# Scans of a four-block image network: where layer norm's factors, their third tile and the squares of x2 are computed

## The chip, the cores and the metric

The kernel runs on one core of a Trainium2 chip, as one program. The metric is device time in microseconds (us), as the median of several executions. The engines are named as the profile names them: PE (TensorE: matmuls, and PEld for its weight loads), DVE (VectorE), ACT (ScalarE), POOL (GpSimd) and SP (SyncE, which issues most DMAs). Each engine takes its own instructions strictly in their order; semaphores join them.

## What is computed

Four residual blocks follow each other on x of 32 x 192 x 56 x 56 numbers in float32: attention with agents, two scans over the pixels (this case), a shift with a small convolution, and a long convolution. The block of the scans, cut to what matters:

```python
k, v, r = (einsum('btc,dc->btd', gn(x), W) for W in (Wk, Wv, Wr))    # b images, t = 3136 pixels, c = 192
x_fwd = wkv_scan(-exp(w_decay), u, k, v)         # y_t = (p + e^(u+k) v) / (q + e^(u+k)), p and q decayed sums
x_bwd = flip(wkv_scan(-exp(w_decay), u, flip(k), flip(v)))
h = sigmoid(r) * 0.5 * (x_fwd + x_bwd)
h = (h - mean_c(h)) * rsqrt(var_c(h) + 1e-5) * ln_g + ln_b           # layer norm over the 192 channels
x2 = x + einsum('btc,dc->btd', h, Wo)            # the next block's group norm needs x2's sums and squares
```

## The kernel before

All of it is in `scan_pairs`. The 32 images are taken as 16 pairs. A pair's 2 x 192 channels lie on three tiles of 128 rows: the first 128 channels of image 0 (tile 0), those of image 1 (tile 1), and the last 64 channels of both, 64 rows each (tile 2, the "third tile"). The 3136 pixels are cut into four pieces m of 784, so one tile is 128 x 784. For a matmul over all channels `_Pairs.outer` (L870) makes tiles 0 and 1, `_Pairs.inner` (L881) the third.

The loop at L1237 runs over the pairs p and, inside, over four steps i. One step does three things:
- `backwards(s, m)` (L1152) for the pair's piece m, from the last piece to the first. For each tile it forms the gate g from Wr (ACT: L1163, L1167, L1168), scans the numerator p and the denominator q from right to left (DVE: two scans L1107, then two scalar_tensor_tensor L1109, here called STT), inverts q on ACT (`inverse`: Ln at L1114, Exp at L1115) and forms h on DVE (L1171 multiplies p by the inverse, L1172 adds the forward part, L1173 multiplies by g).
- `finish` (L1175) for the piece that the step before completed: centred h by PE, its squares on ACT (L1186), their channel mean by PE (`outer` with `mean_w`, so that the mean of both images stands on all 128 rows of two PSUM tiles), the logarithm of variance plus epsilon on ACT (L1195: two of 128 rows for tiles 0 and 1, and two of 64 rows that put the third tile together from both), the exponential that makes it the factor (L1205, three tiles), Wo by PE, the product of both on DVE (L1206), x2 and its sums on DVE (L1207), x2's squares summed on ACT (L1212, into `squares`), and the store of x2 (L1215).
- `forwards(ahead, i)` (L1124) for the next pair's piece i: keys e^k from PSUM on ACT (L1138), values (L1143), the forward scan of the same form, and its quotient y (L1150).

Once in a pair, `moments_of` reads the sums and squares (L1068, L1069), and `conclude` (L1217) finishes the group norm's factors and compares 60 kept maxima with bounds (five L1229, then L1230 takes the smallest).

The order of instructions on each engine is not that of the source: a scheduler orders them when the program is built, by the order of the source and by modelled readiness. It is fixed from then on. PSUM holds four tiles of two banks for all matmuls of the stage (`turned`, L912). SBUF tiles come from pools: x has 7 buffers, ek 12, and g, sq and rd share 8 under the tag "t".

Of the kernel before, what the change touches and what calls it, by code (L numbers as in the profile page):

```python
# [28 lines left out]
C = 192  # L29
# [7 lines left out]
MC = 784  # L37
# [802 lines left out]
class _Pairs:  # L840
# [3 lines left out]
    def __init__(self, nc, pool):  # L844
        self.nc, self.pool = nc, pool

    def blocks(self, name, ap):

        nc = self.nc
        aa = self.pool.tile([128, 128], F32, name=f"{name}_aa", tag=f"{name}_aa")  # L850
        ca = self.pool.tile([128, 128], F32, name=f"{name}_ca", tag=f"{name}_ca")
        ac = self.pool.tile([128, 64], F32, name=f"{name}_ac", tag=f"{name}_ac")
        cc = self.pool.tile([128, 128], F32, name=f"{name}_cc", tag=f"{name}_cc")
        nc.gpsimd.memset(cc, 0.0)  # L854
        nc.sync.dma_start(out=aa, in_=ap[0:128, 0:128])
        nc.sync.dma_start(out=ac, in_=ap[0:128, 128:C])
        for r in (slice(0, 64), slice(64, 128)):
            nc.sync.dma_start(out=ca[r], in_=ap[128:C, 0:128])
            nc.sync.dma_start(out=cc[r, r], in_=ap[128:C, 128:C])
        return aa, ca, ac, cc  # L860
# [32 lines left out]
def scan_pairs(ctx: ExitStack, tc: tile.TileContext, a, k, x1, st_a, st_c, x2, rs2, wogT, count):  # L893
# [6 lines left out]
    NB = x1.shape[0]  # L900
    cp = ctx.enter_context(tc.tile_pool(name="s_c", bufs=1))
    kp = ctx.enter_context(tc.tile_pool(name="s_k", bufs=3 * NM))
    wp = ctx.enter_context(tc.tile_pool(name="s_w", bufs=8))
    sp = ctx.enter_context(tc.tile_pool(name="s_s", bufs=2))
    pp = ctx.enter_context(tc.tile_pool(name="s_p", bufs=4, space=PSUM))
    pairs = _Pairs(nc, cp)
# [10 lines left out]
        return [t[:, h * HM : (h + 1) * HM] for h in range(2)]  # L917


    wo = [small("wo_a", [128, C]), small("wo_c", [64, C])]  # L920
    lg = [small("lg_a", [128, 1]), small("lg_c", [64, 1])]
    lb = [small("lb_a", [128, 1]), small("lb_c", [64, 1])]
    cen = [small("cen_a", [128, C]), small("cen_c", [64, C])]
    for i, r in enumerate((slice(0, 128), slice(128, C))):
        nc.sync.dma_start(out=wo[i], in_=a["L1_conv_WoT"][r])
        nc.sync.dma_start(out=lg[i], in_=a["L1_conv_ln_g"][r].unsqueeze(1))
# [10 lines left out]
    for i, r in enumerate((slice(0, 128), slice(128, C))):  # L937
        n = (128, 64)[i]
        ps, _, _ = turned()
        for s in range(2):  # L940
            nc.tensor.matmul(ps[:n, 0, :C], cen[s][:, r], wo[s], start=(s == 0), stop=(s == 1))
        turn = wp.tile([128, C], F32, name="turn", tag="turn", bufs=1)
        nc.vector.tensor_copy(turn[:n], ps[:n, 0, :C])
        nc.sync.dma_start(out=wogT[r], in_=turn[:n])

    wk, wv, wr = (blocks(n, a[f"L1_conv_{n}T"]) for n in ("Wk", "Wv", "Wr"))
    wog, centre, mean_w, group = (
        blocks("wog", wogT), blocks("cen", k["centre"]), blocks("mean", k["mean192"]), blocks("grp", k["group192"])
    )
    wd = pairs.vector("wd", a["L1_conv_w_decay"])  # L950
    eu = pairs.vector("eu", a["L1_conv_u"])
# [23 lines left out]
    nc.vector.memset(eps, 4.0 * LN_EPS)  # L975
    kept_a, kept_c = small("kept_a", [128, 2, NB // 4, 2]), small("kept_c", [128, 2, NB // 4])
    fine = small("fine", [128, NB // 2])

    def of(t):
        return slice(0, 1) if t < 2 else slice(1, 2)  # L980
# [140 lines left out]
                nc.gpsimd.memset(s, 0.0)  # L1121
        return carry

    def forwards(s, m):  # L1124
        s.ek[m] = [kp.tile([128, MC], F32, name="ek", tag="ek") for _ in range(3)]
        s.bv[m] = [kp.tile([128, MC], F32, name="bv", tag="bv") for _ in range(3)]
        s.y[m] = [kp.tile([128, MC], F32, name="y", tag="y", bufs=3 * NM + 4) for _ in range(3)]
        xn = normed(s, m)
        for tiles in ((0, 1), (2,)):
            for wt in (wk, wv):  # L1130
                ps = [turned() for _ in tiles]
                if len(tiles) == 2:
                    pairs.outer(wt, [q[2] for q in ps], xn)
                else:
                    pairs.inner(wt, ps[0][2], xn)
                for t, (_, both, _) in zip(tiles, ps):
                    if wt is wk:
                        nc.scalar.activation(  # L1138
                            s.ek[m][t].rearrange("p (h n) -> p h n", h=2), both, AF.Exp,
                            accum_out=s.seen[:, 0, 3 * m + t : 3 * m + t + 1],  # L1140
                        )
                    else:
                        nc.vector.tensor_tensor(  # L1143
                            s.bv[m][t].rearrange("p (h n) -> p h n", h=2), both,
                            s.ek[m][t].rearrange("p (h n) -> p h n", h=2), ALU.mult,
                        )
            for t in tiles:
                num, den = scan(s, m, t, s.fore, False)
                inverse(s, den, m, t, 1)
                nc.vector.tensor_tensor(s.y[m][t], num, den, ALU.mult)  # L1150

    def backwards(s, m):  # L1152
        xn = normed(s, m)
        h = s.y[m]
        for tiles in ((0, 1), (2,)):
            ps = [turned() for _ in tiles]
            if len(tiles) == 2:
                pairs.outer(wr, [q[2] for q in ps], xn)
            else:
                pairs.inner(wr, ps[0][2], xn)  # L1160
            for t, (_, both, _) in zip(tiles, ps):
                g = wp.tile([128, MC], F32, name="g", tag="t")
                nc.scalar.activation(  # L1163
                    g.rearrange("p (h n) -> p h n", h=2), both, AF.Exp, scale=-1.0,
                    accum_out=s.seen[:, 3, 3 * m + t : 3 * m + t + 1],
                )
                nc.scalar.activation(g, g, AF.Ln, bias=1.0)  # L1167
                nc.scalar.activation(g, g, AF.Exp, scale=-1.0)  # L1168
                num, den = scan(s, m, t, s.back, True)
                inverse(s, den, m, t, 2)  # L1170
                nc.vector.tensor_tensor(num, num, den, ALU.mult)  # L1171
                nc.vector.tensor_tensor(h[t], h[t], num, ALU.add)  # L1172
                nc.vector.tensor_tensor(h[t], h[t], g, ALU.mult)  # L1173

    def finish(s, m):  # L1175
        h, xs = s.y[m], load(s.p, m)
        hs = [parts(t) for t in h]
        sq = [wp.tile([128, MC], F32, name="sq", tag="t") for _ in range(3)]
# [12 lines left out]
        pv = [turned() for _ in range(2)]  # L1191
        pairs.outer(mean_w, [q[2] for q in pv], sqs)
        rds = [wp.tile([128, MC], F32, name="rd", tag="t") for _ in range(3)]
        for r, t, i, _ in places:
            nc.scalar.activation(rds[t][r].rearrange("p (h n) -> p h n", h=2), pv[i][1][r], AF.Ln, bias=eps[r])  # L1195
        for tiles in ((0, 1), (2,)):
            po = [turned() for _ in tiles]
            if len(tiles) == 2:
                pairs.outer(wog, [q[2] for q in po], hs)
            else:  # L1200
                pairs.inner(wog, po[0][2], hs)
            for t, (_, out, _) in zip(tiles, po):
                rd = rds[t]
                rdh = rd.rearrange("p (h n) -> p h n", h=2)
                nc.scalar.activation(rd, rd, AF.Exp, scale=-0.5)  # L1205
                nc.vector.tensor_tensor(rdh, out, rdh, ALU.mult)  # L1206
                nc.vector.scalar_tensor_tensor(  # L1207
                    xs[t], rd, cb[:, of(t)], xs[t], ALU.add, ALU.add, accum_out=s.sums[:, t, m : m + 1]
                )
                if m == NM - 1:  # L1210
                    nc.vector.tensor_scalar(s.away[:, t], s.sums[:, t, m : m + 1], -1.0 / MC, None, ALU.mult)
                nc.scalar.activation(rd, xs[t], AF.Square, bias=s.away[:, t], accum_out=s.squares[:, t, m : m + 1])  # L1212
        rows = slice(m * MC // S, (m + 1) * MC // S)
        for r, t, i, c in places:
            nc.sync.dma_start(out=x2[c, i, rows, s.p], in_=xs[t][r].rearrange("p (h w) -> p h w", w=S))  # L1215

    def conclude(s):  # L1217
        p = s.p
# [6 lines left out]
        for r, t, i, c in places:  # L1225
            nc.sync.dma_start(out=x2[c, i, S, p], in_=row[r, t])

        for i, top in enumerate((1e8, 1e15, 1e15, 1e15, 1e30)):
            nc.vector.tensor_scalar(s.seen[:, i, :], s.seen[:, i, :], top, None, ALU.is_lt)  # L1229
        nc.vector.tensor_reduce(fine[:, p : p + 1], s.seen.rearrange("p a b -> p (a b)"), AX.X, ALU.min)  # L1230

# [3 lines left out]
    for p in range(NP):  # L1237
        ahead = State(p + 1) if p + 1 < NP else None
        for i in range(NM):
            m = NM - 1 - i  # L1240
            backwards(s, m)
            if i > 0:
                finish(s, m + 1)
            elif before is not None:
                finish(before, 0)
            if ahead is not None:
                forwards(ahead, i)
            if before is not None:
                if i == 1:
                    before.spread = deviations(*moments_of(before), sp, "2")  # L1250
                elif i == 2:
                    conclude(before)
        before, s = s, ahead
    finish(before, 0)
    before.spread = deviations(*moments_of(before), sp, "2")
    conclude(before)
    nc.sync.dma_start(out=rs2[0:128], in_=kept_a)
# [4 lines left out]
    nc.vector.tensor_scalar(eu, eu, 1e8, None, ALU.is_lt)  # L1262
    bad = small("bad", [128, 1])
    nc.vector.tensor_reduce(bad, fine, AX.X, ALU.min)
    nc.vector.tensor_tensor(bad, bad, eu[:, 0:1], ALU.mult)
    nc.vector.tensor_tensor(bad, bad, eu[:, 1:2], ALU.mult)
    nc.vector.tensor_scalar(bad, bad, -1.0, 1.0, ALU.mult, ALU.add)
# [572 lines left out]
```

## Time and profile before

| what | us |
|---|---|
| median of 3 runs (12514.6 to 12529.47) | 12525.27 |
| the profiled execution's own time | 12522.92 |
| its span, first to last instruction | 12521.1 |
| stage of the scans, about 5065 to 8580 of the span | 3515 |
| one step of the stage (53 steps in 5400 to 8300) | 54.7 |
| DVE busy in 7000 to 8000 of the span | 951.9 of 1000 |
| ACT busy there | 670.4 |
| PE busy there | 841.6 |

The page gives busy time in tenths for 40 equal slices of the span; the stage of the scans is slices 17 to 27. A view by windows gives busy time in chosen stretches, a view of waits lists for which instruction of which engine another stood still, and a timeline lists instructions in order of time, with the idle time before each in brackets and the instruction that ended it.

### The profile page before, as it was taken

The page shows a single profiled execution, that of the slowest core. Times are in us where ns is not written, and L with a number is a line of the kernel's source. Part 1 is how long each engine was busy: PE and PEld are TensorE (multiplying, and loading weights), DVE is VectorE, ACT ScalarE, POOL GpSimd, SP SyncE. Part 2 cuts the span into 40 slices and gives each one's busy share as a digit, 9 for nine tenths or more (in the row PEclk, how much of TensorE's full clock was granted, in tenths as well). Part 3 has the DMA queues.
Part 4 walks back from the last instruction along what each step waited for, and adds up shares of the span by engine and source line. Part 5 has one row for each costly group of instructions (what it writes and reads, how often), then busy time and mean ns, then how long its engine had stood idle before and what let it go on. Part 6 is the DMA issues. An engine that isn't in the chain of part 4 may idle for free. (4 is left out here: it accounts for less than half of the span.)

```text
span 12521.1 us, 164987 instructions
## 1 busy us (share of the span) xinstructions
PE 11416.7 (91%) x62738; PEld 7090.4 (57%) x62738; DVE 10875.9 (87%) x15618; ACT 6374.2 (51%) x12012; POOL 2177.8 (17%) x2238
## 2 busy tenths in 40 slices
PE   4999999999999999788888888887999999999999
PEld 1555555555555555333333333335777777777777
DVE  3888888888888888899999999997888888888888
ACT  2555555555555555566666666664333333333333
POOL 0000000000000000555555555552000000000000
PEclk7999999999999999899999999998999999999999
DMA  2111111111111111233333333332111111111111
GB/s 65 36 45 40 40 40 40 39 44 54 40 40 39 40 40 40 74 93 85 86 93 90 83 92 93 86 86 75 43 45 41 44 42 43 43 42 44 42 43 29
DMA packets 930936, 693.89 MB, mean 55 GB/s; under 512 B 775551, under 2 KB 817002, under 8 KB 921121
## 3 DMA queue, kind: packets, MB, share of 16 engines
q1 hardware_dynamic: 930136, 683.25, 21.0%
q8 instruction: 500, 8.19, 0.3%
q14 instruction: 300, 2.45, 0.1%
HBM read 403.18 MB, written 240.80 MB: 51 GB/s over the span
## 5 line engine op out<-in xcount | busy, mean ns | idle before, releaser
L591 DVE SCALAR_TENSOR_TENSOR o<-v_a,dww,o 128x896 f32<-128x896 f32 (+1 forms) x1024 | 1054.0, 1029 | 408.0 <-ACT v_a L565 291.8
L1766 ACT COPY y<-ps 64x252 f32<-64x252 f32 (+1 forms) x2376 | 808.2, 340 | 1134.9 <-PE ps L1760 1104.4
L1684 PE MATMUL ps<-f,real 84*84 84x112 f32 x6144 | 1090.8, 259 | 0.0
L1684 PE MATMUL ps<-f,imag 84*84 84x112 f32 x6144 | 1089.4, 259 | 0.0
L1691 ACT COPY z<-ps 84x448 f32<-84x448 f32 x768 | 405.6, 528 | 1218.0 <-PE ps L1684 1216.4
L1684 PEld LDWEIGHTS ps<-f,real 84*84 84x84 f32 x6144 | 783.9, 153 | 134.2 <-issue 95.8
L854 POOL MEMSET Wk_cc<- 128x128 f32 x1 | 0.2, 204 | 4812.1 <-DVE ones L1269 4812.1
L1684 PEld LDWEIGHTS ps<-f,imag 84*84 84x84 f32 x6144 | 763.8, 153 | 0.0
L1114 ACT ACTIVATE q<-q 128x784 f32<-128x784 f32 x384 | 329.0, 857 | 746.2 <-DVE q L1109 684.3
L591 DVE SCALAR_TENSOR_TENSOR o<-v_c,dww,o 128x448 f32<-128x448 f32 (+1 forms) x1024 | 635.2, 620 | 5.2
L604 PE MATMUL ps<-xs_a,gk_a 128*98 128x448 f32 (+1 forms) x1536 | 639.6, 497 | 0.0
L608 ACT ACTIVATE pr<-ps,low 98x896 f32<-98x896 f32 (+1 forms) x384 | 352.2, 917 | 557.0 <-DVE low L606 557.0
L605 PE MATMUL ps<-xs_c,gk_c 125*98 125x448 f32 (+1 forms) x1536 | 633.1, 493 | 0.0
L696 PE MATMUL ps<-gq_a,xs_a 128*112 128x294 f32 x1792 | 600.5, 416 | 18.8 <-DVE pq L701 18.8
L1701 PE MATMUL ps<-z,f 84*114 84x448 f32 x1536 | 608.9, 539 | 0.0
L697 PE MATMUL ps<-gq_c,xs_c 125*112 125x294 f32 x1792 | 592.9, 411 | 0.0
L1550 POOL TENSOR_TENSOR mat<-tap,tap 114x114 f32<-114x114 f32 x96 | 40.9, 426 | 3166.3 <-PE ps L1610 2313.0
L876 PE MATMUL ps<-sq,mean_aa 128*128 128x392 f32 x512 | 309.2, 748 | 258.6 <-ACT sq L1186 256.6
L1658 PE MATMUL re<-y,f 128*84 128x420 f32 (+1 forms) x1152 | 532.0, 542 | 8.7 <-ACT y L1766 7.6
L709 ACT ACTIVATE pq<-pq 112x1176 f32<-112x1176 f32 x224 | 265.3, 1184 | 530.4 <-DVE pq L701 406.5
L1760 PEld LDWEIGHTS ps<-f,padded 114*128 114x128 f32 x3168 | 473.1, 192 | 96.4 <-issue 70.3
L1658 PE MATMUL im<-y,f 128*84 128x420 f32 (+1 forms) x1152 | 526.9, 538 | 0.0
(398 smaller groups left out, 29528.0 us busy)
## 6 DMA issues: line engine op xcount, KB each, us to landing
x<-x SPq DMA_DIRECT2D x512, 392.0 KB
x<-x SPq DMA_DIRECT2D x512, 196.0 KB
x<-x SPq DMA_DIRECT2D x192, 399.0 KB
out_x<-x SPq DMA_DIRECT2D x384, 196.0 KB
x_a<-in_x SPq DMA_DIRECT2D x32, 1568.0 KB
x<-x_a SPq DMA_DIRECT2D x32, 1568.0 KB
x_c<-in_x SPq DMA_DIRECT2D x64, 392.0 KB
x<-x_c SPq DMA_DIRECT2D x64, 392.0 KB
```

The lines of the kernel that those rows point to most:

```text
L591: nc.vector.scalar_tensor_tensor(dst, tap(i), dww[:, t, i : i + 1], dst, ALU.mult, ALU.add)
L604: mm(ps[P2, h, :n], g[:, cols], xs_a[j][:, px], start=True, stop=False)
L605: mm(ps[P2, h, :n], gk_c[0:KC, 2 * j + h, cols], xs_c[j][0:KC, px], start=False, stop=True)
L608: nc.scalar.activation(pr[:, :, :n], ps[P2, :, :n], AF.Exp, bias=low[:, j, p : p + 1], accum_out=sums[:, j, p : p + 1])
L696: mm(ps[:SUB, i, :HA], xs_a[j][:, px], g, start=True, stop=False)
L697: mm(ps[:SUB, i, :HA], xs_c[j][0:KC, px], gq_c[0:KC, 2 * j + (q + i) // ns], start=False, stop=True)
L1658: nc.tensor.matmul(ps[:, : n * 84], f2[:, i, :], y[:, i0 : i0 + n].rearrange("p g s u -> p (g s u)"), start=True, stop=True)
L1684: nc.tensor.matmul(ps[:84, i * 2 * S : (i + 1) * 2 * S], part[:, i0 + i].rearrange("p s u -> p (s u)"), f3[:, m, :], start=(m == 0), stop= ...
L1691: nc.scalar.copy(z[:, i0 : i0 + n].rearrange("p g m w -> p (g m w)"), ps[:84, : n * 2 * S])
L1701: nc.tensor.matmul(got, f4[:, m, :], z[:, i0 : i0 + n, m, :], start=(m == 0), stop=(m == 1))
L1760: nc.tensor.matmul(ps[:, g * 168 : (g + 1) * 168], flat[:, (g0 + g) * 128 : (g0 + g + 1) * 128], f1, start=True, stop=True)
L1766: nc.scalar.copy(y[64 * m : 64 * m + 64, 2 * g0 + i : 2 * (g0 + n) : 2], got[64 * i : 64 * i + 64, :, :, m, :])
```

## The change

Nothing changes in what is computed. In the loop, `backwards` and `finish` become generators that are advanced in turn: the pair's tiles 0 and 1 backwards, then `finish` up to the factors, then the third tile backwards, then the rest of `finish`. The third tile's factors are no longer computed: the exponentials of tiles 0 and 1 are taken at once, after each logarithm over all 128 rows, and two DMAs on ACT's queue copy rows 0 to 63 of the first and rows 64 to 127 of the second into the third tile. `finish` returns the three squares of x2 uncomputed, and `forwards` issues them behind the first two keys. The product of L1206 goes to the buffer of sq. The five comparisons and the minimum of `conclude` become one instruction with a count. Pool "t" has 9 buffers, ek 13; weights that are used only once are held in "t"; two blocks of `mean_w` that nobody reads are not loaded.

```diff
-    def forwards(s, m):
-        s.ek[m] = [kp.tile([128, MC], F32, name="ek", tag="ek") for _ in range(3)]
+    def forwards(s, m, behind=()):
+        s.ek[m] = [kp.tile([128, MC], F32, name="ek", tag="ek", bufs=3 * NM + 1) for _ in range(3)]
...
+                if wt is wk and tiles == (0, 1):
+                    for later in behind:
+                        later()
...
     def backwards(s, m):
...
                 nc.vector.tensor_tensor(h[t], h[t], g, ALU.mult)
+            yield
...
     def finish(s, m):
...
         rds = [wp.tile([128, MC], F32, name="rd", tag="t") for _ in range(3)]
-        for r, t, i, _ in places:
-            nc.scalar.activation(rds[t][r].rearrange("p (h n) -> p h n", h=2), pv[i][1][r], AF.Ln, bias=eps[r])
+        for t, (_, both, _) in enumerate(pv):
+            nc.scalar.activation(rds[t].rearrange("p (h n) -> p h n", h=2), both, AF.Ln, bias=eps)
+            nc.scalar.activation(rds[t], rds[t], AF.Exp, scale=-0.5)
+
+        for t, r in enumerate((slice(0, 64), slice(64, 128))):
+            nc.scalar.dma_start(out=rds[2][r], in_=rds[t][r])
+        yield
+        left = []
         for tiles in ((0, 1), (2,)):
...
-                nc.scalar.activation(rd, rd, AF.Exp, scale=-0.5)
-                nc.vector.tensor_tensor(rdh, out, rdh, ALU.mult)
+                nc.vector.tensor_tensor(
+                    sq[t].rearrange("p (h n) -> p h n", h=2), out, rds[t].rearrange("p (h n) -> p h n", h=2), ALU.mult
+                )
                 nc.vector.scalar_tensor_tensor(
-                    xs[t], rd, cb[:, of(t)], xs[t], ALU.add, ALU.add, accum_out=s.sums[:, t, m : m + 1]
+                    xs[t], sq[t], cb[:, of(t)], xs[t], ALU.add, ALU.add, accum_out=s.sums[:, t, m : m + 1]
                 )
...
-                nc.scalar.activation(rd, xs[t], AF.Square, bias=s.away[:, t], accum_out=s.squares[:, t, m : m + 1])
+                def square(t=t):
+                    nc.scalar.activation(
+                        sq[t], xs[t], AF.Square, bias=s.away[:, t], accum_out=s.squares[:, t, m : m + 1]
+                    )
+                left.append(square)
...
+        yield left
...
     def conclude(s):
...
-        for i, top in enumerate((1e8, 1e15, 1e15, 1e15, 1e30)):
-            nc.vector.tensor_scalar(s.seen[:, i, :], s.seen[:, i, :], top, None, ALU.is_lt)
-        nc.vector.tensor_reduce(fine[:, p : p + 1], s.seen.rearrange("p a b -> p (a b)"), AX.X, ALU.min)
+        nc.vector.scalar_tensor_tensor(
+            s.seen, s.seen, 1.0, tops, ALU.mult, ALU.is_lt, accum_out=fine[:, p : p + 1]
+        )
...
         for i in range(NM):
             m = NM - 1 - i
-            backwards(s, m)
+            back, ending = backwards(s, m), None
             if i > 0:
-                finish(s, m + 1)
+                ending = finish(s, m + 1)
             elif before is not None:
-                finish(before, 0)
+                ending = finish(before, 0)
+            next(back)
+            if ending is not None:
+                next(ending)
+            next(back)
+            left = next(ending) if ending is not None else []
             if ahead is not None:
-                forwards(ahead, i)
+                forwards(ahead, i, left)
```

## Prediction

> **What bounds the kernel now.** I read the slices first, then busy time by windows in the stage of the scans, then the DVE's waits there, then the timelines of DVE and ACT around each wait. In the slices (tenths busy) the scans are slices 17 to 27. The window's columns are its length, then busy us and instructions of PE, PEld, DVE, ACT and POOL, the granted clock, the DMA share and GB/s.
>
> ```profile
> DVE  3888888888888888899999999997888888888888
> ACT  2555555555555555566666666664333333333333
> ```
> ```profile
> 7000.00:8000.00 1000.00, 841.60 (x2965) 372.96 (x2966) 951.91 (x993) 670.40 (x1126) 525.63 (x501) 0.92 0.36 89
> ```
>
> DVE works 951.9 of 1000 us, PE 841.6, ACT 670.4. So the stage lasts as long as DVE's instructions plus the time DVE stands still. Over 5400 to 8300 (53 steps, 13.25 pairs) its waits are few and named (us in total, times, longest); line numbers are those of the kernel before throughout:
>
> ```profile
> DVE p L1171 <- ACT q L1115: 83.7, 53, 2.3
> DVE q L1107 <- ACT ek L1138: 32.7, 31, 1.2
> DVE mv L1069 <- ACT rd L1212: 12.4, 13, 1.0
> ```
> ```profile
> L1109 DVE SCALAR_TENSOR_TENSOR q<-ek,eu,q 128x784 f32<-128x784 f32 x318 | 324.8, 1025 | 8.7 <-POOL f L1121 0.5
> ```
>
> Per pair that is 6.3 us at L1171, 2.5 at the key scan, 0.95 at L1069, and 0.65 in gaps before an L1109 that follows its own scan directly: 10.4 us, or some 160 us in the stage. This is all that the change can win. The first wait, in one step (DVE, then ACT):
>
> ```profile
> 6037.27 1.04 DVE L1109 SCALAR_TENSOR_TENSOR q<-ek,eu,q 128x784 f32<-128x784 f32 x1
> 6038.22 0.97 DVE L1173 TENSOR_TENSOR y<-y,g 128x784 f32<-128x784 f32 x1
> 6039.10 0.32 DVE L1229 TENSOR_SCALAR seen<-seen 128x12 f32<-128x12 f32 x3
> 6039.34 0.20 DVE L1230 TENSOR_REDUCE fine<-seen 128x1 f32<-128x60 f32 x1
> 6040.87 0.98 DVE L1171 TENSOR_TENSOR p<-p,q 128x784 f32<-128x784 f32 x1 [1.33 <-ACT q L1115]
> ```
> ```profile
> 6038.35 0.86 ACT L1114 ACTIVATE q<-q 128x784 f32<-128x784 f32 x1
> 6039.11 0.89 ACT L1195 ACTIVATE rd<-ps,eps 64x784 f32<-64x784 f32 x1
> 6039.91 0.84 ACT L1115 ACTIVATE q<-q 128x784 f32<-128x784 f32 x1
> ```
>
> DVE hands over the third tile's denominator at 6038.25 and gets the inverse at 6040.87: 2.6 us through Ln, one foreign instruction, Exp. DVE has one 0.88 us instruction to fill them. The second wait: the squares stand ahead of the keys.
>
> ```profile
> 6049.34 0.94 ACT L1212 ACTIVATE rd<-x,away 128x784 f32<-128x784 f32 x1
> 6050.19 0.19 ACT L1212 ACTIVATION_READ_ACCUMULATOR rd<-x,away 128x1 f32 x1
> 6050.40 0.82 ACT L1138 ACTIVATE ek<-ps 128x784 f32<-128x784 f32 x1
> ```
>
> **The change, part by part.** Which instruction fills a wait is decided by the compiled order, which is known for the changed kernel (it has no times). I take spacings from the timelines: scan 1.76 us, STT 0.94, tensor_tensor 0.88, Ln or Exp 0.76, a square with its accumulator 1.1 before a dependent.
>
> *L1171 of the third tile.* In the new order L1173 of tile 1 moves ahead of the last L1109, so it no longer fills the wait; one L1206 takes its place. ACT's order across the wait is L1114, L1167, L1115: again one foreign instruction (0.75 against 0.80 us), so the 2.6 us stay. By the pair's four steps: step 0 has L1206 and the new count (0.2, as L1230) and waits 2.6 - 0.88 - 0.2 = 1.5; step 1 has L1206 and a tiny L1037, 1.6; step 3 L1206 alone, 1.7; step 2 has L1173, the copy of L1224 and two L1206, 2.85 in all, and waits 0. Sum 4.8 against 6.3: 1.5 us per pair won. The change covers this wait in one step of four, not in all.
>
> *Squares.* In the new ACT order two of the three squares still precede the keys in all steps, but one L1206 and one L1207 now follow tile 1's sums on DVE, where mostly one L1207 followed. With tile 1's sums ready at X, the square takes 1.1, the key 0.95 to its reader: the scan can start at X + 2.1. DVE is free at X + 0.95 before (wait 1.15; the trace has 1.15 in each of 26 such steps) and at X + 1.83 after: 0.3. Step 0 adds L1068: 0.05. Step 2 has ACT late by 0.7 us from normalising x (L1089), but L1173 too behind X: 0.2. Step 1 needs L1211 of tile 1, which the new order puts behind the last L1206: 1.0. Sum 1.5 against 2.5: 1.0 won.
>
> *L1069* follows four scan and STT instructions, over 5 us, in the new order; its wait, 0.95 per pair, goes. *L1109*: both scans come before both STTs in every step; the 0.65 goes. The count that replaces L1229 and L1230 lies mostly in the wait just summed; only one L1229 stood outside: 0.1.
>
> Sum: 1.5 + 1.0 + 0.95 + 0.65 + 0.1 = 4.2 us per pair. Some 14.5 of the 16 pairs have this form (the first lacks `finish`, the last `forwards`): 61 us. The set-up loads three blocks less (0.43 + 0.54 + 0.59 on SP) but SP waits up to 1 us longer at the second store of wogT: 0.5, rounded away.
>
> *ACT's work.* Removed per step: two Ln of 64 rows, 0.90 each, and one Exp, 0.84. This frees 2.6 of 54.7 us on an engine that idles for a third: nothing by itself. If it had no idle time left, it would be worth 2.6 us per step.
>
> *The two DMAs on ACT's queue.* No DMA of ACT's is in the trace; the nearest row is SP's loads of x (L997): 319 ns least, 522 median, 1694 most; SP's worst x2 store took 2157. I take 0.5 each. A gain is excluded, since they only add. They wait for the Exp ahead of them, and behind them on ACT stands L1163 of the third tile, then the Ln of L1114 that DVE awaits. From the moment tile 0's denominator is done (0): L1114, L1168, L1115 to 2.6, three L1186 to 5.3, tile 1's inverse 6.4 to 8.25, the mean by PE to 7.9, two Ln to 10.0, two Exp to 11.6; DMAs at 11.8; L1163 is done 1.1 us after them, at about 14. DVE, with 12 instructions between, ends the third denominator at 16.1. Room for both issues together: 3.2 us; in the step kind where one L1186 falls behind tile 1's Ln, 2.1. At 0.5 each it is covered; at 1694 each (3.4) it would cost 0.2 to 1.3 us per step.
>
> A rule speaks against them. The Trainium skill, DMA: Bandwidth & Descriptors, section Rules for kernel authors, says that two transfers to disjoint partition halves do not run side by side but one after the other. The nearest row is wogT (96 KB): issued 5016.25, released its waiter at 5017.99, 1.7 us. Each half here is 200 KB: by the row 1.7 to 3.5 us for both in parallel, by the rule twice that, at most 7. The third tile's L1206 runs 2.6 + 4.5 us after 16.1, so 10 us after the issue. Either way it is hidden.
>
> *What is moved past.* PE now does Wr of the third tile (3.1 us: 1.58 + 1.54 in PE's timeline) between the mean and Wo: Wo's tile 0 comes at 7.9 + 3.1 + 4.1 = 15.3, in the other step kind at 17.0. L1206 is wanted at 16.1, and L1171 behind it waits until 18.7 anyway: no cost. That late Wr also holds two x buffers until 11 to 13, on which SP's loads of the next keys' x wait; the queue has nothing else due then. They are read at 19.6, 7 us later. Startup rows show 1.8 to 2.4 us from issue to waiter for small loads; I allow 4. Covered; without cover, the keys would slip by the excess.
>
> **The rivals.**
> 1. *It covers less than the order suggests.* L1206 itself waits for PE or the factors and pushes L1171, the keys are late as now. Only L1069, the L1109 gaps and 0.1 stay: 1.7 x 14.5 = 25 us, so 12500. For it: three of four steps keep one filler. Against: the room of 1.7 us at L1206.
> 2. *All three waits close*, as the description suggests: 10.4 x 14.5 = 150 us, 12375; half of the difference, 12420, is likelier than the end, if Ln, L1167 and Exp, all from SBUF, pass ACT faster than they do around L1195's read of PSUM. Against: the fixed order of L1114, L1167, L1115.
> 3. *Slower: ACT's queue becomes the bound.* If a DMA on ACT holds its queue over 2.2 us (the longest SP row is 2157 ns) plus 0.5 for the drained pipeline, the pair takes 4.9: late by 1.7 in three steps, 2.8 in one, 2.0 on average. 60 steps x 2.0 = 120 us on top of this sum's 12464: 12584. It eats the gain of 61 us from 1.0 us late on average, at about 1.7 us per DMA with the drain. Against: SP's median of half a microsecond. For it: SP's late loads of x (above) fall into the same two microseconds; if the two queues take turns at issuing, 0.5 becomes 1.0, and 2.0 for both still fits the 2.1 of room.
>
> **How the numbers follow.** Profiled execution 12522.9 - 61 = 12462; the median of the runs lies 2.4 us higher, so 12464. Chances: this sum 0.66, of which 0.02 ends within 0.2%; rival 1 0.10; rival 2 0.17; rival 3 0.07. A measurement can tell about 0.2%, 25 us, from no change. Faster by more: 0.64 + 0.17 + about a quarter of rival 1 = 0.83; same 0.10; slower 0.07. The range runs from 12395 (three quarters of what there is to win) to 12505 (rival 1 and the issue at its dear end): it leaves out rival 3 and the ends of 1 and 2.
>
> **What would show it.** Right: L1171's waits near 70 us over the stage, in three steps of four; the key scan's near 25; L1069 gone from the list; ACT's DMA issues near 0.5 us; L1163 of the third tile ahead of its L1114 with ACT idle between. Wrong: L1163 running into the moment of the third denominator; DVE waiting for PE at L1206 so long that L1171 starts over 2.7 us after it; L1089 waiting for DMA; or L1171 no longer waiting in any step.

## The result and the profile after

The changed kernel takes 12448.08 us (median of 4 runs, 12442.04 to 12455.49) beside 12527.37 us (4 runs, 12514.6 to 12530.93) of the kernel before: ratio 0.9939, 95% interval 0.9922 to 0.9956. It is 79 us faster; 61 were forecast (12464), and the range held the time. The profiled execution has a span of 12447.0 us, 74.1 less than before.

Lines of the changed kernel differ from those of before: L1107, L1109 are now L1118, L1120; L1114, L1115 are L1125, L1126; L1138 is L1149; L1163, L1167, L1168 are L1178, L1182, L1183; L1171 is L1186; L1195 and L1205 are L1212 and L1213; the two DMAs are L1216; L1206, L1207 are L1226, L1229; L1212 is L1236; L1069 is L1080. `outer` ends with L884.

The slices, then the window 7000 to 8000 with the columns as before:

```profile
DVE  3888888888888888799999999997888888888888
ACT  2555555555555555466666666663333333333333
```
```profile
7000.00:8000.00 1000.00, 829.01 (x3034) 378.79 (x3034) 971.09 (x997) 636.59 (x1095) 584.85 (x512) 0.92 0.40 98
```

DVE works 971.1 us of 1000 where it worked 951.9: it still sets the time, and stands still less. DVE's waits over 5400 to 8300 (now 54 steps):

```profile
DVE sq L1226 <- PE ps L884: 47.5, 36, 2.1
DVE p L1186 <- ACT q L1126: 11.8, 21, 1.0
DVE q L1118 <- ACT ek L1149: 10.2, 16, 0.7
DVE sq L1226 <- ACT g L1182: 3.4, 2, 1.7
DVE sq L1226 <- ACT q L1125: 2.7, 3, 0.9
```

The largest wait of before, 83.7 us for the third tile's inverse, is down to 11.8, and an instruction that did not wait before, L1226, waits 53.6. (I count its two rows put down to ACT as PE's: L1226 reads nothing that L1182 or L1125 writes, and in all five of these cases PE ends tiles 0 and 1 of Wo 0.1 us before L1226 starts.) Together that is 65.4 us. The key scan's wait fell from 32.7 to 10.2, and the moments' 12.4 are gone. Here is one step, DVE and then ACT (start, us, engine, line):

```profile
6023.22 1.04 DVE L1120 SCALAR_TENSOR_TENSOR q<-ek,eu,q 128x784 f32<-128x784 f32 x1
6024.17 0.22 DVE L1257 SCALAR_TENSOR_TENSOR seen<-seen,tops 128x60 f32<-128x60 f32 x1
...
6025.06 0.97 DVE L1226 TENSOR_TENSOR sq<-ps,rd 128x784 f32<-128x784 f32 x1 [0.67 <-PE ps L884]
6026.77 0.98 DVE L1186 TENSOR_TENSOR p<-p,q 128x784 f32<-128x784 f32 x1 [0.73 <-ACT q L1126]
```
```profile
6020.16 1.21 ACTq L1216 DMA_DIRECT2D rd<-rd  x2
6021.42 0.82 ACT L1178 ACTIVATE g<-ps 128x784 f32<-128x784 f32 x1 [0.55 <-ACT rd L1213]
...
6024.29 0.86 ACT L1125 ACTIVATE q<-q 128x784 f32<-128x784 f32 x1 [1.96 <-DVE q L1120]
6025.05 0.84 ACT L1182 ACTIVATE g<-g 128x784 f32<-128x784 f32 x1
6025.80 0.84 ACT L1126 ACTIVATE q<-q 128x784 f32<-128x784 f32 x1
```

The third denominator is ready at 6024.2. ACT has the DMAs and L1178 behind it and is idle for 1.96 us, so the queue is not late. Ln, one foreign instruction and Exp take 2.4 us, near the 2.6 of the prediction's chain. DVE starts L1226 in this time, but 0.67 late, because PE brings Wo late; then 0.73 remain at L1186.

To put numbers beside numbers I measure the stage on DVE from the first scan to the last sum of x2. Before: 3510.7 us, of which 179.0 idle. After: 3428.3, of which 112.1 idle. The stage is 82.4 us shorter, 66.9 of it less idle time; the other 15.5 are a closer spacing of the instructions. The stage begins 7.0 us later in the profile after (the attention ahead of it, which is untouched, ends 7.6 us later there), and the rest is 1.3 longer: 82.4 - 8.3 = 74.1, the difference of the spans. Since the start moves by up to 17 us from run to run of the experiments, the stage's length is the finer measure.

### The profile page after: what moved, and what is told of

The parts are those of the page before. It is cut to its first block, busy times and chain, and to the rows that moved or that the text cites. A ratio compares the mean times of both kernels' runs of the same rounds, so it can differ in the third digit from the quotient of the medians.

```text
span 12447.0 us, 164748 instructions
## 1 busy us (share of the span) xinstructions
PE 11356.6 (91%) x62738; PEld 7114.0 (57%) x62738; DVE 10861.2 (87%) x15560; ACT 6217.0 (50%) x11820; POOL 2303.7 (19%) x2237
## 3 DMA queue, kind: packets, MB, share of 16 engines
q1 hardware_dynamic: 929832, 683.18, 21.3%
## 5 line engine op out<-in xcount | busy, mean ns | idle before, releaser
L1125 ACT ACTIVATE q<-q 128x784 f32<-128x784 f32 x384 | 328.7, 856 | 808.9 <-DVE q L1120 637.8
L1801 PEld LDWEIGHTS ps<-f,padded 114*128 114x128 f32 x3168 | 473.3, 192 | 96.7 <-issue 70.3
L1801 PE MATMUL ps<-f,padded 114*128 114x168 f32 x3168 | 503.7, 310 | 21.6 <-DVE o L1744 10.2
```

The lines of the kernel that those rows point to most:

```text
L1801: nc.tensor.matmul(ps[:, g * 168 : (g + 1) * 168], flat[:, (g0 + g) * 128 : (g0 + g + 1) * 128], f1, start=True, stop=True)
```

## Experiments

All are the changed kernel with an edit, each timed in turn with the kernel before (whose median was 12515 to 12526 us in those series); medians are of five runs, of 16 for no_weave and of four for warm_products_half. The stage comes from one trace of each. What they compute is unchanged, but for the idle matmuls of the warm ones, whose result is overwritten.

| kernel | median us | ratio, 95% interval | stage us | idle in it |
|---|---|---|---|---|
| before | 12527.37 | | 3510.7 | 179.0 |
| changed | 12448.08 | 0.9939 (0.9922 to 0.9956) | 3428.3 | 112.1 |
| squares_ahead | 12467.16 | 0.9952 (0.9938 to 0.9965) | 3449.6 | 124.4 |
| no_weave | 12501.73 | 0.998 (0.9973 to 0.9988) | 3485.1 | 169.0 |
| no_transfer | 12458.89 | 0.9949 (0.9935 to 0.9962) | 3449.7 | 133.8 |
| four_transfers | 12447.97 | 0.9938 (0.9925 to 0.9952) | 3432.9 | 122.1 |
| gate_early | 12421.97 | 0.9919 (0.9906 to 0.9933) | 3405.1 | 97.0 |
| products_first | 12418.29 | 0.9915 (0.9902 to 0.9929) | 3404.5 | 92.7 |
| both | 12421.82 | 0.9918 (0.9905 to 0.9932) | 3404.9 | 96.7 |
| warm | 12795.56 | 1.0222 (1.0208 to 1.0236) | | |
| warm_products | 12785.1 | 1.0215 (1.0201 to 1.0229) | | |
| warm_half | 12447.91 | 0.9938 (0.9925 to 0.9952) | 3436.1 | 123.0 |
| warm_products_half | 12402.96 | 0.9904 (0.9889 to 0.9919) | 3385.8 | 74.2 |

The first four edits ask what carries the gain; the others ask what DVE waits for now. An edit also lets the scheduler order the engines anew, so each has to be read with the order that its trace shows.

**squares_ahead.** x2's squares go back to their old place, ahead of the next keys.

```diff
-                left.append(square)
+                square()
```


> The changed kernel with x2's squares issued at their old place, ahead of the next pair's keys. Theory (the squares' place is worth what the prediction gave to the key scan and to L1069, 1.0 + 0.95 us per pair, times 14.5 pairs): about 28 us slower than the changed kernel, 12476 us, the key scan's wait back near 2 us per pair and a wait of the moments for ACT back in the list. Rival (the waits only change places, since DVE waits for PE at the next product anyway): within 8 us of 12448.

Measured: 19 us slower than changed, 21.3 in the stage. The size is near the first theory's 28, and its mechanism is refuted. Over the stage the key scan waits 12.0 us (changed 10.9) and L1080 does not wait at all. What came back is another thing, seen in DVE's timeline:

```profile
6093.80 1.03 DVE L1120 SCALAR_TENSOR_TENSOR q<-ek,eu,q 128x784 f32<-128x784 f32 x1
6094.75 1.85 DVE L1118 TENSOR_TENSOR_SCAN q<-decay,f,ek 128x784 f32<-128x784 f32 x1
6096.70 1.04 DVE L1120 SCALAR_TENSOR_TENSOR q<-ek,eu,q 128x784 f32<-128x784 f32 x1
```

The order now puts an STT directly behind the scan whose result it reads, as before. From a scan's start to the next start it is 1.953 us in these 92 cases of the stage (changed has 4), and 1.742 where the STT belongs to another scan. 92 x 0.21 = 19 of the 21.3 us. The rest of DVE's order in a step is that of the changed kernel. So moving the squares is worth about 20 us by the scan order that comes with it; why the scheduler chooses it is not shown.

**no_weave.** The third backward tile is issued as a whole ahead of the layer norm's factors.

```diff
             next(back)
+            next(back)
             if ending is not None:
                 next(ending)
-            next(back)
```


> The changed kernel with the whole of the third backward tile issued ahead of the layer norm's factors, all else as changed. Theory (the place of the factors between second and third tile is what closes a part of the wait for the third inverse and keeps the factors off it): the 1.5 us per pair of the prediction come back, 12470 us; if DVE then waits for the factors at its first product, which come after mean, two Ln and two Exp, up to 12520. Rival (the place is worth nothing, the gain is the squares' and the sums' order): within 8 us of 12448.

```profile
DVE p L1186 <- ACT q L1126: 56.8, 38, 2.4
DVE q L1118 <- ACT ek L1149: 34.7, 27, 1.9
DVE sq L1226 <- PE ps L884: 26.4, 16, 2.2
DVE mv L1080 <- ACT sq L1236: 12.7, 14, 0.9
```

54 us slower than changed, 56.8 in the stage, where I had 22 and at most 72. All three waits of before are back: 83.2 us in the third tile, 34.7 at the key scan, 12.7 at the moments. Yet the squares are still issued behind the keys here. What the edit changes on DVE is two of the four steps of a pair, 0 and 2, which go back to the order that before has around the third tile; there lie the moments' wait and the key scan's new one (1.9 us in each step 2). Steps 1 and 3 keep the changed order and, at the key scan, its waits. So the key scan and the moments are covered by the order of products and sums that the interleaving brings, not by where the squares stand. The 26 us that are left of the gain are near the 25 of the prediction's first rival by chance: that rival keeps the moments' gain, which is lost here, and gives L1109 half of what it is worth.

**no_transfer and four_transfers.** In the first, the third tile's factors are computed again; in the second each DMA becomes two of 32 rows.

```diff
-            nc.scalar.dma_start(out=rds[2][r], in_=rds[t][r])
+            nc.scalar.activation(rds[2][r]..., pv[t][1][r], AF.Ln, bias=eps[r])
+        nc.scalar.activation(rds[2], rds[2], AF.Exp, scale=-0.5)
```
```diff
-            nc.scalar.dma_start(out=rds[2][r], in_=rds[t][r])
+            for q in (slice(r.start, r.start + 32), slice(r.start + 32, r.stop)):
+                nc.scalar.dma_start(out=rds[2][q], in_=rds[t][q])
```


> The changed kernel with the third tile's factors computed again on ACT (two Ln of 64 rows and an Exp, 2.6 us) where the two transfers are issued (0.47 us each). ACT is 1.7 us later with the third tile's gate and inverse. Theory (ACT has 2 to 3 us of room there, so neither the removed work nor the transfers carry any of the gain): within 12 us of 12448. Rival (the work taken from ACT is what the gain comes from): 1.7 us in each of 60 steps, 100 us slower, 12550.

> The changed kernel with each of the two transfers of the third tile's factors cut into two of 32 rows, so that ACT issues four DMAs where it issued two: 0.94 us more of ACT's time ahead of the third tile's gate. Theory (the room on ACT is 2.1 to 3.2 us, of which two issues take 0.9): within 8 us of 12448. Rival (ACT's queue is at its limit there): 0.94 us in each of 60 steps, 56 us slower, 12504.

ACT's DMA issues, changed and then four_transfers (ns least, median, longest):

```profile
L1216 ACTq DMA_DIRECT2D rd<-rd x108: 468/468/1640, 5435.4 to 8263.0; - x108
```
```profile
L1217 ACTq DMA_DIRECT2D rd<-rd x216: 513/597/1164, 5425.6 to 8259.8; - x108
```

From the first issue to the end of the last, four take 2.5 to 2.8 us in 40 of 54 steps and 4.2 to 5.1 in the others, against 1.2 for two in nearly all steps. The median is the same all the same; in the stage's length it is 4.6 us. But this does not show that the issues are free: ACT, which in the changed kernel idles 0.4 to 2.2 us ahead of the third tile's Ln in 53 of 54 steps, does not idle there in 42 of 54 now, and the scheduler gave DVE another order: in three steps of four both products and sums of tiles 0 and 1 stand ahead of L1186, as in gate_early below, which takes 12422. no_transfer has the same difficulty. It is 11 us slower than changed, 21.4 in the stage:

```profile
5961.84 0.82 ACT L1178 ACTIVATE g<-ps 128x784 f32<-128x784 f32 x1
5962.68 0.20 ACT L1178 ACTIVATION_READ_ACCUMULATOR g<-ps 128x1 f32 x1
5962.79 0.84 ACT L1217 ACTIVATE rd<-rd 128x784 f32<-128x784 f32 x1
5963.54 0.84 ACT L1182 ACTIVATE g<-g 128x784 f32<-128x784 f32 x1
5964.28 0.84 ACT L1125 ACTIVATE q<-q 128x784 f32<-128x784 f32 x1
```
```profile
5964.28 1.86 DVE L1227 TENSOR_TENSOR sq<-ps,rd 128x784 f32<-128x784 f32 x2 [1.60 <-PE ps L884]
5966.74 0.98 DVE L1186 TENSOR_TENSOR p<-p,q 128x784 f32<-128x784 f32 x1 [0.60 <-ACT q L1126]
```

No idle time is left ahead of L1125: the third denominator is ready at 5962.7, and its Ln starts 1.6 us later, where the changed kernel started it at once. On DVE, though, two products stand ahead of L1186 where the changed kernel has one (the products are L1227 here). That is the order of products_first below, the same in three steps of four, and that order alone gains 30 us. Beside products_first, no_transfer is 41 us slower, 45 in the stage. So the 11 us are a difference of two effects: behind this order the removed work, less the two issues, is worth some 40 us, not nothing, and still less than half of the rival's 100.

**gate_early, products_first, both.** The first emits the third tile's gate (3.1 us of PE) ahead of the factors, so that PE does Wo sooner. The second lets DVE do the products of tiles 0 and 1 ahead of the last three instructions of the third tile, and their sums behind these. The third does both. Their cores:

```diff
+        gate((2,))
         yield
-        gate((2,))
         num, den = scan(s, m, 2, s.back, True)
```
```diff
         inverse(s, den, m, 2, 2)
+        yield
         rest(2, num, den)
```


> The changed kernel with the third tile's gate (Wr by PE, its tanh on ACT) issued ahead of the layer norm's factors, so that PE does Wo 3 us earlier; on DVE the products and sums of tiles 0 and 1 then stand ahead of the third tile's product with its inverse. Theory (PE's late Wo is what DVE waits for, 1.2 us per step, and the third inverse is covered by two products and two sums): the waits for PE and for the inverse, 65 us over 54 steps, mostly close, 40 to 60 us faster than 12448: 12390 to 12410. Rival A (PE is late because it was idle before, not because of the order; then the wait for PE stays, and the tile-2 inverse's goes): 12435. Rival B (the wait at the moments returns and ACT's factors now come later than PE): 12448 or slower.

> The changed kernel with DVE's last three instructions of the third backward tile issued behind the products of tiles 0 and 1 with their factors; PE's order is untouched. Theory (PE's Wo is what comes late): DVE still waits for PE at the product of tile 0, and only what waited for the inverse (11.8 us in 54 steps) goes: within 15 us of 12448. Rival (the inverse, not PE, sets the end): 40 us or more faster.

> The changed kernel with both edits: the third tile's gate ahead of the factors, and its last three DVE instructions behind the products of tiles 0 and 1. Theory (the two do not add: with PE early, the order on DVE is already that of the gate's edit alone): as with the gate alone, 12390 to 12410. Rival (each closes its own wait): faster than the gate alone by over 10 us.

(The gate's part on ACT is Exp, Ln and Exp, not a tanh.) DVE's waits of gate_early (L1226 is L1241 there):

```profile
DVE sq L1241 <- PE ps L884: 35.7, 29, 1.7
DVE q L1118 <- ACT ek L1149: 27.6, 27, 1.0
```

and of products_first:

```profile
DVE sq L1241 <- PE ps L884: 54.5, 41, 1.8
DVE q L1118 <- ACT ek L1149: 4.4, 14, 0.3
```

26 and 30 us faster than changed; both together are no more than gate_early alone, as expected, since the order on DVE is the same in both. My sizes missed in both: gate_early gained less than 40, because the wait for PE fell by a third only and the keys' wait rose from 10.2 to 27.6; products_first gained twice the 15 that I allowed: with the inverse's wait (11.8) half of the keys' wait went too, 17.6 us together in this window (the whole stage is 24 shorter). In products_first nothing waits for the inverse any more, and the wait for PE is as large as ever. So PE's lateness is real, and I asked what causes it.

**warm, warm_products, warm_half, warm_products_half.** In the changed kernel PE waits for the squares of L1203 and then takes the mean. PE's timeline, and two windows (granted clock third from the end):

```profile
6011.52 4.59 PE L881 MATMUL ps<-sq,mean_aa 128*128 128x392 f32 x8 [8.83 <-ACT sq L1203]
6016.04 1.59 PE L884 MATMUL ps<-sq,mean_ca 64*128 64x392 f32 x8
```
```profile
6011.00:6015.00 4.00, 3.48 (x6) 1.90 (x7) 4.00 (x5) 2.59 (x7) 3.83 (x3) 0.50 0.00 0
6015.00:6020.00 5.00, 5.00 (x22) 2.19 (x22) 5.00 (x6) 3.64 (x6) 4.75 (x4) 1.00 0.00 0
```

After 8.83 us of rest the clock granted is 0.50, and the eight matmuls take 4.59 us, 4.3 to 5.6 over the steps with 6.6 or 8.8 us of rest, where the same form takes 2.90 with Wk or Wv. This is what the Trainium skill, TensorE: Matmul & The Clock Gate, section Part 1: The HAM clock gate, describes: the array runs at half clock after an idle window and gets the full clock after a time of work. The edit fills the rest with matmuls into the PSUM tile that the mean overwrites.

```diff
+        for _ in range({0: 22, 1: 16, 2: 0, 3: 22}[m]):
+            nc.tensor.matmul(pv[0][2][0], mean_w[0], hs[0][0], start=True, stop=True)
         pairs.outer(mean_w, [q[2] for q in pv], sqs)
```


> The changed kernel with 16 or 22 matmuls more on PE ahead of the mean, in three steps of four (none in the step where PE waits only 2.4 us there). They write the mean's own PSUM tile, which the mean then overwrites, and fill the 6.6 to 8.8 us in which PE waits for the squares and after which the trace shows the mean at a granted clock of 0.50 (4.5 to 5.6 us where the same eight matmuls of the keys take 2.9). Theory (the late product of DVE comes from PE's halved clock after its idle time): the mean takes 2.9 us, Wo comes 1.6 to 2.7 us sooner in three steps of four, DVE's wait for PE, 61 us in the stage, mostly closes; what then waits is the third tile's inverse behind one product, as the prediction had it (some 0.5 to 1 us per step less than now): 15 to 40 us faster than 12448, 12410 to 12435. Rival (the clock is nothing to the end: DVE only waits for the inverse instead): within 8 us of 12448. Third possibility (the filling matmuls hold PE up): slower.

> The same filling matmuls in the kernel whose third backward tile ends behind the products of tiles 0 and 1 (12418 us without them). There DVE waits for PE alone, 60 us in the stage. Theory (PE's halved clock after idle): most of that goes, 30 to 50 us faster, 12370 to 12390. Rival (PE's order, the third tile's gate ahead of Wo, is what makes it late): within 10 us of 12418.

They are 347 and 367 us slower than the kernels they were built from. I had taken each filling matmul at half of its time: 16 of them (32 instructions in the trace) took 10.8 us and 22 took up to 16.5, and the fill ran into the mean. The third possibility came true, by my sizing. But the mean behind them took 2.80 us. So again with eight (5.5 us, 7.2 in some steps), `{0: 8, 1: 8, 2: 0, 3: 8}`:

> The changed kernel with eight filling matmuls ahead of the mean in three steps of four (0.67 to 0.73 us each as the longer fill showed, so 5.4 to 5.9 us; the longer fill was twice what fits and held PE up). They lie in the 6.6 us in which PE waits for the squares with a free PSUM tile. Theory (DVE waits for PE's Wo because the mean runs at half clock after the idle time): the mean takes 2.8 to 2.9 us, it and Wo come 1.7 to 2.7 us sooner in three steps of four; DVE's wait for PE, 61 us in the stage, falls by half or more; part of it comes back as a wait for the third tile's inverse behind one product, which the prediction priced at 4.8 us per pair: between nothing and 25 us faster than 12448. Rival (the clock is nothing to the end): DVE's wait for PE stays, within 8 us of 12448.

> The same eight filling matmuls in the kernel whose third backward tile ends behind the products of tiles 0 and 1 (12418 us without them), where DVE in the third tile waits for PE alone, 60 us in the stage. Theory (PE's halved clock): Wo 1.7 to 2.7 us sooner in three steps of four, most of the 60 us goes: 25 to 50 us faster than 12418, 12370 to 12395. Rival (the place of the third gate's matmuls ahead of Wo is what makes it late): the wait stays, within 8 us of 12418.

PE in warm_half at the same step:

```profile
6001.92 5.54 PE L1210 MATMUL ps<-y,mean_aa 128*128 128x392 f32 x16 [2.37 <-ACT g L1178]
6008.38 2.90 PE L881 MATMUL ps<-sq,mean_aa 128*128 128x392 f32 x8 [0.93 <-ACT sq L1203]
```

DVE's waits in warm_half (L1226 is L1228 there), and the step again:

```profile
DVE p L1186 <- ACT q L1126: 62.2, 40, 1.6
DVE q L1118 <- ACT ek L1149: 10.1, 15, 0.7
DVE sq L1228 <- PE ps L884: 2.5, 2, 1.3
```
```profile
6021.18 0.97 DVE L1228 TENSOR_TENSOR sq<-ps,rd 128x784 f32<-128x784 f32 x1
6023.63 0.98 DVE L1186 TENSOR_TENSOR p<-p,q 128x784 f32<-128x784 f32 x1 [1.48 <-ACT q L1126]
```

In this window the wait for PE is gone, 53.6 to 2.5, and the time is the same to 0.2 us: the wait stands at L1186 now, 1.48 where the changed kernel had 0.67 + 0.73 = 1.40. In warm_products_half, where the inverse has two products for cover, the fill gains 15 us in the medians, 18.7 in the stage:

```profile
DVE p L1188 <- ACT q L1126: 27.8, 41, 0.7
DVE q L1118 <- ACT ek L1149: 4.2, 14, 0.3
```

(L1186 is L1188 there.) 27.8 us turn up at the inverse, 0.7 at most each. I had expected 25 to 50, and up to the last pair it is so: the last pair's first backward scan comes 32.6 us sooner after the stage's start than in products_first, and in warm_half 8.1 us sooner than in changed. The last pair gives 14 and 16 us back. Over 8440 to 8530, which holds its end, DVE's wait for PE in changed and in warm_half is:

```profile
DVE sq L1226 <- PE ps L884: 15.7, 2, 9.1
```
```profile
DVE sq L1228 <- PE ps L884: 29.8, 2, 17.9
```

No keys of a next pair follow there, the rest that the fill was sized for is missing in part, and the fill stands in PE's way; leaving it out of the last pair was not tried. By the medians the two edits give 0, 30 and 45 us: the fill alone, the order alone, both; up to the last pair 8, 24 and 56. In the changed kernel DVE waits for whichever is later, PE's Wo or the inverse behind one product, and in the step shown the two lie within a microsecond of each other. gate_early, products_first and both beat the changed kernel, and warm_products_half is the fastest of all.

## Why the prediction was right

The terms over the stage, forecast (its sum per pair times 14.5) and measured in the traces, both in us. The measured ones are counted from the first scan to the last scan, where the stage is 84.8 us shorter.

| term | forecast | measured |
|---|---|---|
| third tile's wait, L1171 | 22 | 91.9 to 75.3 (12.8 at L1186, 59.1 at L1226 and L1229, 3.4 once at L1154): 16.6 |
| count | 1.5 | 10.7 to 3.4: 7.3 |
| key scan | 14.5 | 39.2 to 10.9: 28.3 |
| L1069 | 13.8 | 13.3 to 0: 13.3 |
| L1109 behind its own scan | 9.4 | gaps 9.1, scans' spacing 8.0: 17.1 |
| sum | 61 | 82.6 |

- **L1171.** The decisive choice was that the wait is set by the chain Ln, one foreign instruction, Exp, and that the change covers one step in four. The total is right: 65.4 us over 54 steps is 4.8 per pair, the forecast's number, and so is its split. In pairs 1 to 14 the waits at L1226 and L1186 together are 1.54, 1.59, 0.08 and 1.70 us in steps 0 to 3, where 1.5, 1.6, 0 and 1.7 were forecast; in warm_half, without the wait for PE, L1186 alone has 1.49, 1.56, 0 and 1.63. Where it shows was wrong: the prediction called PE's Wo no cost because L1171 waits behind it anyway. warm_half shows that it costs next to nothing here, 8 us over fifteen pairs; that L1226 carries most of the visible wait I did not forecast. The mis-sized term is the mean by PE. The prediction has it end 7.9 us behind tile 0's denominator and Wo at 15.3; in the step shown the denominator is ready at 6008.19, the mean ends at 6017.63 and Wo at 6024.96, 9.4 and 16.8 us behind it. The trace of before had the slow mean already: 4.6 to 6.0 us for these eight matmuls after 4.2 to 4.4 us of rest. With the count, 23.9 us against 23.5: fewer comparisons mostly lengthen the wait that they lay in.
- **Key scan: mis-sized, the largest error.** I had the scan waiting 0.05 to 0.3 us in three steps and 1.0 in one. It waits 0.7 in the step with the extra L1211 (now L1233) and practically not in the others. In a step without the wait, tile 1's sums end at 5979.30, ACT's square and key are done at 5981.26, and DVE, with L1226 and L1229 of the third tile, starts the scan at 5981.30: 2.0 us of work where I had 1.83, against 1.96 needed where I had 2.1. They cross by hundredths of a microsecond, so that the wait goes altogether there is luck. And no_weave and squares_ahead show that the part's name "Squares" was wrong: the order of products and sums covers this wait.
- **L1069** went as forecast, 13.3 for 13.8; it too belongs to the interleaving (no_weave has 12.7 of it back).
- **L1109: mis-sized by half.** I counted the gaps that the profile marks, 8.7 us in the window, and not that the scan ahead of such an STT is itself followed 0.1 us later. In before 87 cases stand at 1.957 us from start to start against 1.742. The gap was half of the cost.
- **ACT's work and queue.** "Nothing by itself" for the removed work is not what the runs show: 11 us (no_transfer beside changed), some 40 where DVE's order is the same (beside products_first). The sum did not miss it, since its waits were worked out in the changed kernel's order, where that work is gone. The DMAs at 0.5 us each were right, 468 ns, and cheaper than that for ACT: the first is issued beside the second Exp, so both leave ACT idle for 0.55 us only, the second issue included. Rival 3 needed over 1.7 us each; the longest of all took 1.64.
- **The rule on partition halves** that spoke against the DMAs: the third tile's L1226 never waits for them in the stage. In the last step, where no keys follow, the two were issued from 8493.00 on and the product that reads them started at 8498.55, behind other work and without a wait. So both, 196 KB each, landed within 5.5 us. Whether they overlapped is not settled by this; no product of the stage waited for it.
- **The late x loads: the margin was wrong.** I had 7 us. SP does wait longer for the buffers, and ACT then waits for x in 14 of 54 steps, once per pair, 0.65 us on average and 0.9 at the longest, which before it did in none. It was one of the signs that I had named for "wrong". It costs little: nearly all of these waits lie in the step after the one with the 0.7 us at the key scan, and there DVE does not wait for the keys.

Of the rivals, 1 matches no_weave in number alone. 2 would have needed all three waits to close: two of them nearly did, and the largest did not. Its likelier 12420 is what products_first reaches with an order that the change does not have.

## What to carry to other kernels

When a wait shrinks and another appears on the neighbouring instruction, two chains end at nearly the same time, and an edit to one of them shows less than it is worth: the fill gave 8 us over fifteen pairs alone and 33 on top of the new order. Before an edit's size is read, compare the compiled order of the engine that bounds: no_transfer was to change ACT's work alone, DVE's order moved with it, and 30 of its 41 us were hidden. An idle gap in front of an instruction is not the whole cost of a dependence; compare start to start with the same instruction elsewhere. An interleaving is to be costed by the new order on the engine that bounds, not by the parts that its description names.

## What the runs showed of the hardware that was not expected

- PE's mean takes 4.3 to 5.6 us instead of 2.9 after 6.6 to 8.8 us of rest, at a granted clock of 0.50 where it was read. After 2.4 us of rest, four of these matmuls took 1.58 us in some steps and 2.98 in others. With a fill of 5.5 to 7.2 us in the rest, the mean behind it took 2.8 to 2.9 in every step of the window; a fill of 10.8 to 16.5 us cost 347 and 367 us.
- An STT directly behind the scan that it reads costs 0.21 us more, 0.1 of it as a gap, on a scan of 1.74 us.
- A DMA issue on ACT takes 468 ns at the median (1640 at the longest); of four back to back the median was 597 each. Two cost ACT 0.55 us of idle time, as the first ran beside an Exp.
